# Gated cross-attention and ternary FFN: tokens of six batches read channel first and normalised in place, output weight issued by ScalarE, products and bank reads listed separately

## The chip, the cores and the metric

The program runs on one core of one Trainium2 chip. The metric is device microseconds (us) of one execution: the median of 3 runs, 726.65 us before the change (724.81 to 727.16). The profile is one further execution of the same kernel, which took 723.52 us, 721.7 us of them inside the recorded span.

Engines: PE (TensorE, matmuls; PEld is its weight load), DVE (VectorE), ACT (ScalarE), POOL (GpSimd) and SP (SyncE, which here only issues transfers). Each engine takes its instructions in order. [...]

## What is computed

Eight batches of 512 tokens with 512 channels go through two residual steps.

```python
x = x + tanh(g_xattn) * xattn(layernorm(x), ctx, mask, Wq, Wk, Wv, Wo, ...)
x = x + tanh(g_ffn) * ffn(layernorm(x), gate_w, val_w, out_w, ...)

# xattn: 16 heads of 32 channels, 64 context tokens per batch
q, k, v = proj(hs, Wq, bq), proj(at, Wk, bk), proj(at, Wv, bv)
probs = softmax(clip(mask(q @ k.T / sqrt(32))))
delta = layernorm(clip(rs, 0, 0.3) * ((probs @ v) @ Wo.T + bo)) * ln_gamma + ln_beta

# ffn: 512 -> 2 x 2048 -> 512; activations rounded to 8 bits per token, weights to -1, 0, 1
h = silu(bit_linear(x, gate_w)) * bit_linear(x, val_w)
out = bit_linear(h, out_w)
```

## The kernel before

The 4096 tokens are 32 tiles of 128 tokens; batch b has four (ST = 4). The common path (`common_path`) is one straight program. The lists of calls in `opening`, `attend_third`, `attend` (batches 3 to 6), `attend_last` and `closing` set the order, and `in_order` (L75) fixes it: on each engine, instructions stand exactly as the calls issued them. The sequencers wait for semaphores only.

Stages of the attention of batch b (counted from 0):

- `load_x` (L136) loads a tile of x, tokens on partitions. `ln1_stats` (L200) takes mean and variance per token on DVE and 1/sqrt on POOL.
- `ln1` (L222) writes the normalised tile `hs` on DVE (L230) and adds the output shift to x on POOL (L220). `ln1_turn` (L237) turns `hs` to channels on partitions: four PE transposes through the identity into one PSUM bank (L247), and one ACT copy into `hT` (L248). `hT` has one buffer for 512 tokens.
- `queries(b, o)` (L252): four f32 products from `hT` into a bank, then ACT writes `qT` (L263).
- `scores(b, a)` (L276): eight small products into four banks (L288), then ACT takes Exp of each into `prob` (L297). Exp and Silu each have to be loaded into ACT's table when it last did the other.
- `sums` (L303) adds the probabilities on PE (L311); ACT copies them (L317), and SP sends them through DRAM to 128 rows (L319, L321). `spread` (L324) takes the reciprocal on DVE and sends it through DRAM into `R` (L331, L337).
- `values` (L342): products (L351), then DVE multiplies by `R` (L358). `project_out(b, t)` (L370): four f32 products into a bank (L375), then four DVE instructions (L382 to L386). `add_delta` (L388) scales and adds into x.

Stages of the FFN of one tile: `ffn_stats` (L546), in six steps for a batch; `ffn_in` (L603) rounds a tile and turns it by a transposing DMA (L611); `ffn_mid(b, i, jj)` (L615), half of the hidden width: 4 bias products and 16 products into four banks (L625, L630), then Silu on ACT (L636) and a product on DVE (L637) for each of two column blocks; `ffn_quant` (L650), the row maximum on DVE (L655); `ffn_quant2` (L668), which rounds on ACT and DVE (L673, L674) and turns by two transposing DMAs (L679); `ffn_out` (L682): 16 products into one bank (L690), a DVE instruction (L697) and the store (L698). `tile_in`, `tile_mid`, `tile_max`, `tile_quant` and `tile_out` do the next of these for the tiles in order, so the FFN of batch b-1 runs between the attention stages of batch b.

The eight banks are two pools of four: `four` for `ffn_mid`, and `bank` for nearly all else. A bank is given on when its reader has finished. All transfers are issued by SP, the ternary weights among them: `ternary_load` (L437) brings 1 MB quarters of the gate, value and output weight during the opening, five buffers in all; `magnitude` sums them and `ternary` (L479) makes -1, 0 and 1 of them on ACT (L489, L490) or DVE (L493, L494).

## Time and profile before

| what | us |
|---|---|
| median of 3 runs | 726.65 |
| profiled execution, whole | 723.52 |
| its span | 721.7 |
| PE busy in the span | 693.5 |
| DVE / ACT / POOL busy | 519.2 / 372.0 / 133.4 |
| first matmul starts | 4.33 |
| first `ffn_mid` of the kernel starts | 132.82 |
| `attend` for one of batches 3 to 6 | 83 |
| last matmul ends | 716.05 |

In the profile, part 1 gives the busy time of each engine. The timeline lists an engine's instructions in order of time, runs of equal ones merged, and in square brackets how long the engine was idle just before and what released it. The chain of waits is followed back from the last instruction. The granted TensorE clock was 1.00 in every stretch up to 690 us and 0.96 after it.

### The profile page before, as it was taken

To read this page: it belongs to the slowest core of one execution; us is meant where nothing else is said; L and a number is where in the kernel's file an instruction comes from. 1 tells how busy PE (TensorE), PEld (TensorE's weight loads), DVE (VectorE), ACT (ScalarE), POOL (GpSimd) and SP (SyncE) were. 2 spreads that over 40 slices of the span, in tenths; PEclk is the share of its full clock that TensorE was granted. 3 is DMA by queue.
4 is the path that set the end of the run, shared out by engine and by line. 5 is a ranking of instruction groups with operands and counts; after the bars stand their busy time and mean duration, and the time that the engine had idled before them with its cause. 6 is when DMAs were issued, how large, how long until landed. Compare 5 with 4: busy or idle time off the path is not lost.

```text
span 721.7 us, 9373 instructions
## 1 busy us (share of the span) xinstructions
PE 693.5 (96%) x3292; PEld 288.6 (40%) x3292; DVE 519.2 (72%) x973; ACT 372.0 (52%) x477; POOL 133.4 (18%) x195
## 2 busy tenths in 40 slices
PE   7999899989999999999999999999999899999996
PEld 3544344334443434443443434443443334433343
DVE  3578879877687757685767957686676659888773
ACT  0569855567137663268326583077524652355551
POOL 1072303114011510043001321024000021003000
PEclk9999999999999999999999999999999999999999
DMA  8975612123322433124530525113320332233543
GB/s 275 407 245 198 208 33 88 25 67 98 88 44 56 108 76 96 36 40 96 106 84 12 106 61 132 37 38 76 86 63 15 70 97 44 53 86 75 88 80 93
DMA packets 114249, 68.36 MB, mean 95 GB/s; under 512 B 97489, under 2 KB 97489, under 8 KB 113169
## 3 DMA queue, kind: packets, MB, share of 16 engines
q1 hardware_dynamic: 114192, 67.67, 36.4%
q8 instruction: 28, 0.46, 0.3%
q14 instruction: 29, 0.23, 0.1%
HBM read 36.71 MB, written 8.91 MB: 63 GB/s over the span
## 4 chain that ended last, share of the span: by engine, by line
PE 55%; DVE 15%; issue 3%; DMA 2%; ACT 1%; POOL 1%; SPq 0%; DVEq 0%; ACTq 0%
PE four L630 19%; PE bank L690 12%; PE bank L375 10%; PE bank L258 6%; DVE h_g L655 3%; DVE h L637 2%; PE bank L630 2%; PE bank L311 2%; PE four L625 2%; DVE ln_st L558 1%; DVE x L399 1%; DVE hs L230 1%; PE bank L288 1%; PE bank L351 1%; DVE ln_st L211 1%
## 5 line engine op out<-in xcount | busy, mean ns | idle before, releaser
L636 ACT ACTIVATE gate<-four,sgv 128x512 f32<-128x512 f32 x112 | 74.9, 683 | 138.1 <-PE four L630 137.8
L630 PEld LDWEIGHTS <-xqT 128*128 128x128 bf16 x1024 | 94.9, 98 | 124.2 <-issue 15.8
L673 ACT ACTIVATE h<-h,magic,h_s 128x1024 f32<-128x1024 f32 x64 | 75.9, 1234 | 92.8 <-DVE h_s L662 92.8
L690 PE MATMUL bank<-out_tern,hqT 128*128 128x512 fp8e4 x512 | 115.4, 379 | 6.6 <-DMA hqT<-hq 3.3
L375 PE MATMUL bank<-wo_sb,cT 128*128 128x512 f32 x256 | 113.9, 596 | 3.9 <-DVE cT L358 3.2
L630 PE MATMUL four<-gate_tern,xqT 128*128 128x512 fp8e4 x448 | 115.6, 381 | 1.4 <-DMA xqT<-xq 1.4
L258 PE MATMUL bank<-hT,wq_sb 128*128 128x512 f32 x256 | 115.9, 600 | 0.4 <-ACT hT L248 0.4
L630 PE MATMUL four<-val_tern,xqT 128*128 128x512 fp8e4 x448 | 115.0, 379 | 0.0
L637 DVE SCALAR_TENSOR_TENSOR h<-four,sgv,gate 128x512 f32<-128x512 f32 x112 | 81.0, 746 | 28.1 <-PE four L630 21.4
L690 PEld LDWEIGHTS <-hqT 128*128 128x128 bf16 x512 | 49.9, 98 | 70.7 <-issue 9.8
L375 PEld LDWEIGHTS bank<-wo_sb,cT 128*128 128x128 f32 x256 | 48.1, 190 | 63.5 <-issue 51.5
L258 PEld LDWEIGHTS bank<-hT,wq_sb 128*128 128x128 f32 x256 | 47.2, 190 | 64.0 <-issue 55.6
L655 DVE TENSOR_REDUCE h_g<-h 128x1 f32<-128x2048 f32 (+1 forms) x32 | 71.6, 2238 | 0.3
L664 POOL TENSOR_TENSOR so<-h_g,unit 128x1 f32<-128x1 f32 x32 | 6.6, 205 | 297.9 <-DVE h_g L660 288.0
L220 POOL TENSOR_TENSOR x<-x,bet_bc 128x512 f32<-128x512 f32 x32 | 46.2, 1464 | 69.3 <-DVE hs L230 44.5
L674 DVE TENSOR_SCALAR hq<-h 128x1024 bf16<-128x1024 f32 x64 | 43.3, 693 | 21.4 <-ACT h L673 20.1
L569 POOL TENSOR_TENSOR x<-x,ob_bc 128x512 f32<-128x512 f32 x32 | 40.0, 1282 | 44.2 <-ACT h L568 44.2
L382 DVE TENSOR_TENSOR d<-bank,bo_bc 128x512 f32<-128x512 f32 x32 | 22.0, 687 | 26.8 <-PE bank L375 26.8
L263 ACT ACTIVATE qT<-bank,bq_sb 128x512 f32<-128x512 f32 x32 | 22.0, 688 | 36.0 <-PE bank L258 36.0
L697 DVE SCALAR_TENSOR_TENSOR o<-bank,so,x 128x512 f32<-128x512 f32 x32 | 24.0, 749 | 20.9 <-PE bank L690 18.3
L609 DVE TENSOR_SCALAR xq<-h 128x512 bf16<-128x512 f32 x32 | 13.5, 423 | 33.7 <-ACT h L606 33.7
L606 ACT ACTIVATE h<-h,magic,ln_r 128x512 f32<-128x512 f32 x32 | 25.7, 807 | 13.8 <-DVE ln_r L583 13.8
(137 smaller groups left out, 740.2 us busy)
## 6 DMA issues: line engine op xcount, KB each, us to landing
x<-in_x SPq DMA_DIRECT2D x32, 256.0 KB
R<-over SPq DMA_DIRECT2D x64, 128.0 KB
out_x<-o SPq DMA_DIRECT2D x32, 256.0 KB
wraw<-in_gate_w SPq DMA_DIRECT2D x4, 1024.0 KB
wraw<-in_val_w SPq DMA_DIRECT2D x4, 1024.0 KB
wraw<-in_out_w SPq DMA_DIRECT2D x4, 1024.0 KB
cT_in<-in_cxT SPq DMA_DIRECT2D x4, 256.0 KB
wk_sb<-in_wk SPq DMA_DIRECT2D x4, 256.0 KB
```

Of the source, the lines that this page charges most:

```text
L220: nc.gpsimd.tensor_tensor(src, src, bet_bc, ALU.add)
L258: nc.tensor.matmul(ps, wq_sb[:, c, o * P : (o + 1) * P], hT[:, c, :], start=(c == 0), stop=(c == DC - 1),)
L375: nc.tensor.matmul(ps, st_[b, "cT", c][:, t * P : (t + 1) * P], wo_sb[:, c, :], start=(c == 0), stop=(c == DC - 1),)
L569: nc.gpsimd.tensor_tensor(xs, xs, ob_bc, ALU.add)
L606: nc.scalar.activation(h2, h2, AF.Identity, scale=s[:, i : i + 1], bias=magic)
L630: nc.tensor.matmul(ps, xqT[:, c, :], w[:, c, cols], start=False, stop=(c == DC - 1))
L636: nc.scalar.activation(gate, four[2 * k], AF.Silu, scale=sgv[:, 0, i : i + 1])
L637: nc.vector.scalar_tensor_tensor(h[:, cols], four[2 * k + 1], sgv[:, 1, i : i + 1], gate, ALU.mult, ALU.mult)
L655: nc.vector.tensor_reduce(gx, h if part is None else h[:, F // 2 :], AX.X, ALU.max, apply_absolute_value=True)
L673: nc.scalar.activation(h[:, cols], h[:, cols], AF.Identity, scale=s, bias=magic)
L674: nc.vector.tensor_scalar(hq, h[:, cols], MAGIC, None, ALU.subtract)
L690: nc.tensor.matmul(ps, hqT[:, c % (FC // 2), :], weights["out"][:, c, :], start=(c == 0), stop=(c == FC - 1),)
```

## The change

- **Tokens channel first.** The kernel has a further input, `xT`, x with channels ahead of tokens. For batches 2 to 7 (the third to the eighth) `ln1` and `ln1_turn` are gone. `load_turned(b)` loads `hT` straight from `xT` by four transfers of 256 KB. `ln1_stats` keeps mean and 1/sqrt side by side (one small DVE copy more). `ln1_rows(b)` writes them to DRAM as two rows of 512, and reads each back into all 128 partitions. `ln1_turned` subtracts the mean row from `hT` on DVE in one instruction of 128x2048, `ln1_turned_end` multiplies by the other row on POOL in two of 128x1024. x itself is still loaded, for statistics and residual. Batches 0 and 1 are transposed as before.
- **Second queue.** The four 1 MB quarters of `out_w` are issued by ACT; everything else stays on SP.
- **Reads apart from products.** Nearly every helper that issued products and read their banks is split in two (`queries` and `queries_end`, `scores` and `scores_end`, `ffn_mid` and `ffn_gate`, `ffn_out` and `ffn_end`, and so on; `ffn_quant2` takes one half at a time), and all lists of calls are written anew, the start of the kernel and `closing` too.

```diff
+    def ln1_rows(b):
+        rows = dram.tile([2, S], F32, tag="lnrows", name="lnrows")
+        nc.sync.dma_start(
+            out=rows.rearrange("r (t p) -> p r t", p=P), in_=st_[b, "ln1"][1]
+        )
+        for i in range(2):
+            row = work.tile([P, S], F32, tag="hs", name="row", bufs=2)
+            nc.sync.dma_start(out=row, in_=rows[i].partition_broadcast(P))
+            st_[b, "row", i] = row
+
+    def load_turned(b, queue=nc.sync):
+        hT = st_[b, "hT"] = work.tile([P, DC, S], F32, tag="hT", name="hT")
+        for c in range(DC):
+            queue.dma_start(
+                out=hT[:, c, :], in_=xT[c * P : (c + 1) * P, b * S : (b + 1) * S]
+            )
+
+    def ln1_turned(b):
+        hT, m = st_[b, "hT"], st_[b, "row", 0].unsqueeze(1)
+        nc.vector.tensor_tensor(hT, hT, m.to_broadcast([P, DC, S]), ALU.subtract)
+
+    def ln1_turned_end(b):
+        hT, r = st_[b, "hT"], st_[b, "row", 1].unsqueeze(1)
+        for h in range(2):
+            half = hT[:, h * DC // 2 : (h + 1) * DC // 2, :]
+            nc.gpsimd.tensor_tensor(half, half, r.to_broadcast([P, DC // 2, S]), ALU.mult)
...
-            nc.sync.dma_start(
+            (nc.scalar if name == "out" else nc.sync).dma_start(
                 out=raw.rearrange("p (c n) -> p c n", c=per),
```

The list of `attend(b)` afterwards, one line for each stretch:

```python
add_scaled(b-1, 0, 1); tile_mid; sums(b, 0); queries(b, 2); sums_end(b, 0); tile_gate
queries_end(b, 2); tile_in; spread(b, 0); add_scaled(b-1, 2, 3); spread_end(b, 0)
load_turned(b+1); queries(b, 3); tile_mid; ln1_rows(b+1); tile_gate; tile_max
queries_end(b, 3); values(b, 0); values_end(b, 0); tile_mid; tile_gate; scores(b, 1)
ffn_stats(b-1, 0); ffn_stats(b-1, 1); scores_end(b, 1); tile_quant; tile_quant; tile_out
load_x; tile_in; tile_mid; tile_end; tile_gate; ln1_turned(b+1); ln1_turned_end(b+1)
tile_max; sums(b, 1); tile_out; sums_end(b, 1); ffn_stats(b-1, 2); tile_mid; tile_end
tile_gate; spread(b, 1); tile_quant; load_x; ffn_stats(b-1, 3); tile_quant
queries(b+1, 0); queries(b+1, 1); queries_end(b+1, 1); queries_end(b+1, 0)
ffn_stats(b-1, 4); ffn_stats(b-1, 5); tile_in; tile_mid; spread_end(b, 1); tile_gate
tile_max; tile_out; tile_end; values(b, 1); load_x; values_end(b, 1); tile_quant; tile_mid
tile_quant; scores(b+1, 0); ln1_stats(b+2, 0); add_beta(b+1, 0..3); project_out(b, 0)
scores_end(b+1, 0); tile_gate; load_x; project_out(b, 1); project_end(b, 0); tile_in
ln1_stats(b+2, 1); tile_out; pair_up(b+1); tile_end; ln1_stats(b+2, 2); project_end(b, 1)
tile_mid; tile_gate; project_out(b, 2); tile_max; project_end(b, 2); project_out(b, 3)
tile_quant; tile_quant; project_end(b, 3); check_sums(b); delta_scale(b); ln1_stats(b+2, 3)
```

`add_scaled` and `delta_scale` are `add_delta` in two parts. `scores(b+1, 0)`, which opened the next `attend` before, now stands ahead of `project_out(b, 0)`.

## The prediction, as it was recorded

> **What bounds the kernel now.** First the busy times in part 1 of the page, which tell which engine can set the end:

> ```profile
> PE 693.5 (96%) x3292; PEld 288.6 (40%) x3292; DVE 519.2 (72%) x973; ACT 372.0 (52%) x477; POOL 133.4 (18%) x195
> ```

> PE is idle for 28.2 of 721.7 us, 4.3 of them ahead of its first matmul and 5.7 behind its last. So the kernel gets shorter by what leaves PE's list and by stalls between matmuls, and by little else. I therefore read PE's waits next (total us, times, longest):

> ```profile
> PE bank L690 <- DMA hqT<-hq: 3.3, 2, 2.5
> PE bank L375 <- DVE cT L358: 3.2, 2, 2.0
> PE bank L690 <- ACT x L297: 2.2, 1, 2.2
> PE bank L247 <- DVE o L697: 1.9, 4, 0.5
> PE bank L247 <- DVE hs L230: 1.6, 3, 1.0
> ```

> The two L247 lines are the transposes' own waits. Then the groups by shape (busy, mean ns | idle before):

> ```profile
> L311 PE MATMUL bank<-prob,ones 64*32 64x512 f32 x208 | 20.7, 600 | 0.0
> L247 PE MATMUL bank<-ident,hs 128*128 128x128 f32 x128 | 18.3, 279 | 4.1 <-DVE o L697 1.9 <-DVE hs L230 1.6 <-ACT qT L263 0.3
> ```

> A transpose takes 18.3 / 128 = 0.143 us of PE. The line of the sums hides something: the list of waits has none for it, yet the timeline of PE over one attend (start, us) shows two lengths for the same 16 products:

> ```profile
> 308.54 1.09 PE L311 MATMUL bank<-prob,ones 64*32 64x512 f32 x16
> ...
> 326.99 0.66 PE L247 MATMUL bank<-ident,hs 128*128 128x128 f32 x4 [0.48 <-DVE o L697]
> ...
> 336.39 2.73 PE L311 MATMUL bank<-prob,ones 64*32 64x512 f32 x16
> ```

> The second, 2.73 against 1.09, is a stall of 1.64 that counts as busy. ACT's timeline says why: the scores end at 332.5, but ACT comes to their Exps late, and these last until 338.0:

> ```profile
> 333.92 1.28 ACT L297 ACT_TABLE_LOAD   x1
> 335.22 2.78 ACT L297 ACTIVATE prob<-bank,esh,esc 128x512 f32<-128x512 f32 x4
> ```

> Last, one stretch of one period of the attention (start:end, length, then busy time of PE, PEld, DVE, ACT, POOL):

> ```profile
> 303.79:386.96 83.17, 82.69 (x408) 34.26 (x408) 58.77 (x114) 42.46 (x57) 15.90 (x23) 1.00 0.35 73
> ```

> The other engines have 24 us or more to spare in each period. There are four such, so a us in each is worth four.

> **Transposes.** Six batches lose 16 each: 96 x 0.143 = 13.7 of busy time. In a period the records overlap their neighbours (three spans of 1.04, 0.66 and 0.66 take 2.12 between starts), so 6 x 2.12 = 12.7; I take **-13**. Their waits leave with them: 1.9 (o), 1.3 of 1.6 (hs; the rest is in batches 0 and 1) and 0.3 (qT): **-3.5**. After them the same out follows a mid, whose 3.9 us let DVE finish o, so nothing takes their place.

> **The norm that replaces them.** Off PE: it loses on ACT four copies (L248) of 0.59, and on DVE four L230 of 0.54. It gains:
> - Four loads of 256 KB per batch, in place of none. They stand on SP's queue and wait for the last queries of batch b, which read the one hT. Behind them on SP stand the two rows' transfers and the next transposes of hq, which are due some 11 us later. An issue takes SP 0.43, 1.7 for four; DMA is busy 0.35 of the period. Cost: nothing; if the cover were gone, 1.7 per batch.
> - The rows: a write of 1,024 pieces of 4 bytes, which the trace does not show, then reads. Nearest are SP's waits for the rows of sums and of reciprocals, 30.7 / 16 = 1.9 in the mean and 6.3 at most. The subtract comes about 17 us after; I take 1.9 and nothing at either end.
> - One subtract of 128x2048 on DVE. Below: four L230, 2.1; above: four L386 (two tensors read, 0.752), 3.0. I take 2.25, nearer to L230; DVE's sum is then as before.
> - Two POOL products of 128x1024. L220 has two inputs from SBUF and ranges 1.26 to 3.32 for 512: 4 x 1.27 = 5.1 at the least, 4 x 3.32 = 13.3 at the most. I take 5.1, as L220's median is 1.36.

> When is hT needed? On PE, the sums (1.0), an out (3.5) and a mid (3.9) stand between the mid ahead of the subtract and the queries of b+1: 8.4. The chain is the gate's last DVE product (0.86), subtract (2.25) and products (5.1): 8.2. The second half is needed only 1.7 later. So **0**, with little slack for the first half and 2 for the second.

> [...]

> **Sums apart from scores.** In the new list an out and a mid (7.4 us) stand between scores(b, 1) and sums(b, 1), so Exp has ended: 4 x 1.64 = **-6.6**. But an out then directly follows the scores, and scores(b+1, 0) are directly followed by project_out(b, 0). Scores fill all four banks of their pool, so the next product waits until the first Exp has read its bank. The row that shows such a case is in the last attention:

> ```profile
> 574.14 3.61 PE L690 MATMUL bank<-out_tern,hqT 128*128 128x512 fp8e4 x16 [2.19 <-ACT x L297]
> ```

> Below, the wait is 0.9: Exp starts 0.2 after the scores' end (304.66 to 304.86) with the table loaded ahead, and one takes 0.70. Above, the table load (1.28) and a tile's rounding (2.37) stand before it: 4.6. In the list both ACT entries ahead are a gate's Silu, as at 304.86, so I take 1.0 for each: two in each of four attends, one in the third, 9 x 1.0 = **+9**. In the last attention the 2.19, and 0.9 by which the scores ahead are slow (1.95 in place of 1.11), become 2.0: **-1.1**.

> **Single waits.** The first out waits 2.54 for hqT at 156.84; it moves behind a mid (3.9): **-2.5**. The cT wait of 1.20 at 595.1 goes, as another product is put between: **-1.2**.

> **The opening and the second queue.** The other cT wait, 2.0 at 86, follows a transfer of R that landed 6.3 late behind 2 MB of output weight issued just ahead of it. With the weight on ACT it is issued at other times: **-1** (between 0, when it lands among the same transfers, and -2). ACT pays 0.4 to 0.5 for each issue, and may wait at its head for the ternary value weight; Exps stand behind. In the opening ACT is the less loaded, so 0.

> [...]

> **Sum:** -13 - 3.5 - 6.6 + 9 - 1.1 - 2.5 - 1.2 - 1 = -19.9. From the profiled 723.5 that gives 703.6; the median shown lies 3.1 above that execution, so 706.8. I say **706**. By stage: each attend 83.2 to 81 (-2.1 of transposes, -0.5 of waits, -1.64, +2), the third 6 less, the opening 1 to 3 less.

> **Rivals.**
> - *A, the Exp is late.* At one scores of each attend ACT still has the table load and a rounding ahead, as at 333.92: 3.65 more each, 4 x 3.65 = +14.6: 720. For it: the old list shows just that at the second half, and DVE makes the gates late. Against: in the new list the roundings stand behind scores_end. 0.18; spans 712 to 724.
> - *B, slower: the norm is late.* If the POOL pair is near its 13.3, the chain is 0.86 + 2.25 + 13.3 = 16.4 against 8.4 + 1.7 of cover: 6.3 per batch, x 6 = 38: 744. With the chain 3.4 beyond the cover, a pair of 10.4, it costs 20 and decides; above that the kernel is slower. For it: the 3.32 of L220, and DVE 70% busy. Against: the median of 1.36. 0.12.
> - *C, nothing.* B at that point, a pair of 10.4: the norm gives back just what the transposes and stalls gave, 726. 0.04.
> - *D, more.* The waits for banks are hidden, +9 gone: 697. PE's other idle between matmuls is 28.2 - 4.3 - 5.7 = 18.2, of which the steps above take 9.3; were the rest gone too, 688. 0.06.

> **Chances.** Forecast 0.60 (699 to 712), A 0.18, B 0.12, C 0.04, D 0.06. A difference below 0.3% (2.2 us) is about what a measurement of this kernel cannot tell from none. Faster: 0.60 + 0.18 + 0.06 = 0.84; within 0.3%: 0.04; slower: 0.12. The range takes the forecast, most of A and half of D: 694 to 722.

> **What would show it.** Right: L247 falls to 32 instructions; the period is about 81; the sums take 1.09 throughout; PE's list has an L690 and an L375 line released by Exp (L297 before), about 1.0 each; queries wait for POOL under 0.3. Wrong: queries wait for POOL's products by several us (B), the bank waits are 3 or more (A), or PE waits in the opening for weights that ACT issued late, which I put at nothing.

## The result and the profile after

The changed kernel takes 751.88 us in the median (751.42 to 759.47, 4 runs) against 725.73 us: 1.0383 of the time, 95% interval 1.0314 to 1.0452. I had forecast 706, range 694 to 722. The profiled execution took 751.72 us, with a span of 749.9 us against 721.7.

Part 1 of its page, and the lines of PE's waits that matter (total us, times, longest):

```profile
PE 690.7 (92%) x3196; PEld 280.4 (37%) x3196; DVE 537.2 (72%) x961; ACT 361.1 (48%) x453; POOL 168.0 (22%) x207
```

```profile
PE bank L757 <- DMA hqT<-hq: 14.7, 5, 4.1
PE bank L331 <- DVE cT L417: 10.5, 1, 10.5
PE bank L433 <- DVE cT L417: 4.9, 2, 4.2
...
PE bank L757 <- ACT prob L344: 4.3, 5, 0.9
PE bank L433 <- ACT prob L344: 3.6, 4, 0.9
```

PE lost 96 transposes, yet it is busy for only 2.8 us less, and idle for 59.2 us in place of 28.2. The two lines released by `prob` are the nine bank waits that the prediction counted, 7.9 in place of 9. The first two lines, 25.2 us, are what it did not have. L757 is an out (the products of `ffn_out`), L331 a scores, and `hqT` and `R` (for `cT`) are brought by transfers.

So the next view is the list of what SP's queue waited for:

```profile
SPq L749 <- DVE hq L744: 72.7, 27, 9.1
SPq L229 <- DMA lnrows<-ln_r: 57.0, 6, 11.8
```

L229 reads the rows back. It waits six times, 9.5 us in the mean, for the write of the 1,024 numbers that stands just ahead (L224). SP's queue in one attention (start, us) shows who stands behind it:

```profile
339.41 0.38 SPq L224 DMA_DIRECT2D lnrows<-ln_r  x1
348.57 0.80 SPq L229 DMA_DIRECT2D row<-lnrows  x2
349.48 4.93 SPq L749 DMA_TRANSPOSE hqT<-hq  x2
```

The write is issued at 339.4, the reads can go at 348.6, and only then come the two turns of hq (transposing transfers into hqT), which take 4.9 to issue beside half a MB of rows. DVE writes the two halves of hq at:

```profile
347.74 0.69 DVE L744 TENSOR_SCALAR hq<-h 128x1024 bf16<-128x1024 f32 x1 [0.34 <-ACT h L743]
348.87 0.69 DVE L744 TENSOR_SCALAR hq<-h 128x1024 bf16<-128x1024 f32 x1 [0.43 <-ACT h L743]
```

So here the first half had been ready for 1.1 us when its turn was issued; in the other three attentions it was 2.1, 4.5 and 3.5. In the two attentions where hq had waited least, the pair of turns took 4.9 and 4.6 to issue, against 2.6 or 2.7 for most pairs of the kernel before. hqT is late by both: the wait, and the half MB that it puts right ahead of the turns. On PE, from one scores of the period to the next, with the sums and the out that needs hqT:

```profile
298.50 1.11 PE L331 MATMUL bank<-qT,kT 32*64 32x512 f32 x16
...
342.54 1.22 PE L331 MATMUL bank<-qT,kT 32*64 32x512 f32 x16
...
352.05 1.09 PE L358 MATMUL bank<-prob,ones 64*32 64x512 f32 x16
355.65 5.31 PE L757 MATMUL bank<-out_tern,hqT 128*128 128x512 fp8e4 x16 [2.51 <-DMA hqT<-hq]
...
383.89 1.11 PE L331 MATMUL bank<-qT,kT 32*64 32x512 f32 x16
```

The sums now take 1.09, as forecast. The out waits 2.51, and then takes 5.31 in place of 3.6: from 356 to 358 us the granted clock is 0.50, from 358 to 360 it is 0.69. Without these 4.2 us the period, 85.4 between the scores at 298.50 and at 383.89, would be 81.2.

In the third attention the same wait holds up the second transfer of batch 2, R:

```profile
151.42 0.39 SPq L224 DMA_DIRECT2D lnrows<-ln_r  x1
160.26 0.80 SPq L229 DMA_DIRECT2D row<-lnrows  x2
161.15 2.43 SPq L392 DMA_DIRECT2D R<-over  x4
```

```profile
159.53 1.07 PE L331 MATMUL bank<-qT,kT 32*64 32x512 f32 x4
171.08 2.59 PE L331 MATMUL bank<-qT,kT 32*64 32x512 f32 x12 [10.48 <-DVE cT L417]
```

The values of batch 2 hold two banks until R is there, so the scores stand still for 10.5 us.

By stage, in us, as differences from the kernel before (first column), with the kernel of the experiments that turns the statistics on PE (called "turned rows" below) in the last column. The forecast's terms are put to the stages here; for the third attention the prediction itself had said "6 less".

| stage | before | forecast | after | turned rows |
|---|---|---|---|---|
| start to the first `ffn_mid` | 132.8 | -3.1 | +5.7 | +5.3 |
| to the scores of batch 3 | 87.7 | -5.5 | +10.2 | -1.6 |
| to the last scores | 349.5 | -9.0 | +11.2 | -7.4 |
| to the end of the span | 151.7 | -2.3 | +1.1 | -0.5 |
| sum | 721.7 | -19.9 | +28.2 | -4.2 |

### The profile page after: what moved, and what is told of

Read it like the earlier page. It is cut to its first block, busy times and chain, and to the rows that moved or that the text cites. A ratio compares the mean times of both kernels' runs of the same rounds, so it can differ in the third digit from the quotient of the medians.

```text
span 749.9 us, 9162 instructions
## 1 busy us (share of the span) xinstructions
PE 690.7 (92%) x3196; PEld 280.4 (37%) x3196; DVE 537.2 (72%) x961; ACT 361.1 (48%) x453; POOL 168.0 (22%) x207
## 4 chain that ended last, share of the span: by engine, by line
PE 72%; DMA 12%; DVE 9%; ACT 3%; issue 2%; SPq 1%; POOL 1%; DVEq 0%; ACTq 0%
PE four L696 24%; PE bank L757 14%; PE bank L433 12%; PE bank L295 9%; DMA hqT<-hq 4%; PE bank L696 3%; PE four L691 2%; PE bank L780 2%; PE bank L331 2%; DMA R<-over 2%; DMA rows<-den 1%; PE bank L794 1%; PE bank L406 1%; DMA lnrows<-ln_r 1%; DMA wo_sb<-in_wo 1%
## 5 line engine op out<-in xcount | busy, mean ns | idle before, releaser
L757 PE MATMUL bank<-out_tern,hqT 128*128 128x512 fp8e4 x512 | 125.2, 401 | 21.9 <-DMA hqT<-hq 14.7
L707 DVE SCALAR_TENSOR_TENSOR h<-four,sgv,gate 128x512 f32<-128x512 f32 x112 | 81.2, 747 | 68.6 <-PE four L696 38.7
L757 PEld LDWEIGHTS <-hqT 128*128 128x128 bf16 x512 | 51.8, 102 | 99.4 <-issue 30.2
L744 DVE TENSOR_SCALAR hq<-h 128x1024 bf16<-128x1024 f32 x64 | 50.7, 806 | 15.2 <-ACT h L743 12.4
L261 POOL TENSOR_TENSOR x<-x,bet_bc 128x512 f32<-128x512 f32 x32 | 50.2, 1597 | 18.2 <-DVE bet_bc L177 17.5
L255 POOL TENSOR_TENSOR hT<-hT,row 128x1024 f32<-128x1024 f32 x12 | 28.4, 2388 | 79.4 <-DVE hT L247 69.7
L344 ACT ACTIVATE prob<-bank,esh,esc 128x512 f32<-128x512 f32 x40 | 27.9, 778 | 21.0 <-PE bank L331 21.0
L196 POOL TENSOR_TENSOR ln_r<-ln_r,mhalf 128x4 f32<-128x4 f32 x16 | 16.5, 1032 | 80.8 <-DVE ln_r L195 46.5
## 6 DMA issues: line engine op xcount, KB each, us to landing
wraw<-in_gate_w SPq DMA_DIRECT2D x4, 1024.0 KB, 12.2
```

The costliest lines, as they stand in the source:

```text
L255: nc.gpsimd.tensor_tensor(half, half, r.to_broadcast([P, DC // 2, S]), ALU.mult)
L261: nc.gpsimd.tensor_tensor(src, src, bet_bc, ALU.add)
L707: nc.vector.scalar_tensor_tensor(h[:, cols], four[2 * k + 1], sgv[:, 1, i : i + 1], gate, ALU.mult, ALU.mult)
L744: nc.vector.tensor_scalar(hq, h[:, cols], MAGIC, None, ALU.subtract)
L757: nc.tensor.matmul(ps, hqT[:, c % (FC // 2), :], weights["out"][:, c, :], start=(c == 0), stop=(c == FC - 1),)
```

## The experiments

**Theory W:** the write of 1,024 pieces holds SP at the reads' wait, and what is queued behind is late. Rivals: T, traffic of rows and xT; L, the new lists; A, the output weight on ACT. (These letters, and Q, E and R below, are not the prediction's rivals A to D.)

### Rows read later

```diff
+        ln1_rows_end(b + 1)      # the two reads, now behind the turns of hq
         tile_out()
```

> The changed kernel with one move: the reads of the two rows are issued by SP later, behind the turns of hq (in the opening behind the sums of batch 1), the write stays where it is. Theory W (SP stands 8.3 to 11.8 us at the reads' wait for the write of 1,024 pieces, and all that is queued behind it is late): the stall of 10.5 at 160 goes, the four waits for hqT (13.3 in all) fall under 1 each, the half clock after them goes; 700 to 712 us. Rival T (not the wait, but the rows' and xT's traffic keeps hqT and R late): the reads still run beside the turns; over 735. Rival L (the new lists themselves put outs ahead of their hqT): over 730, the stall at 160 stays.

Measured: 733.09 us, 1.0102 of before (1.0061 to 1.0143). The waits for hqT in the attentions are gone and the period is 81.7, but the stall in the third attention is still 6.7, and the one ahead of the first projection is 5.6, and the time is over the 700 to 712 expected. W is half right. The trace tells what it lacked:

```profile
152.04 0.39 SPq L224 DMA_DIRECT2D lnrows<-ln_r  x1
153.04 1.71 SPq L398 DMA_DIRECT2D R<-over  x4
```

R was issued 1 us behind the write and ahead of the reads, so SP did not stand at the write first. Its last part still landed 12.7 us after its issue (2.9 in the median of those that the trace shows), while the view of the transfers shows 0 to 55 GB/s until 163.6 us. So in this run the write delayed transfers, not only the queue.

### The write in 128 pieces

```diff
-            out=rows.rearrange("r (t p) -> p r t", p=P), in_=st_[b, "ln1"][1]
+            out=rows.rearrange("r (p k) -> (r p) k", k=2 * ST),
+            in_=st_[b, "ln1"][1].rearrange("p r t -> p (r t)"),
```

> The changed kernel with the write of mean and 1/sqrt in 128 pieces of 32 bytes in place of 1,024 of 4, so the rows hold the numbers at wrong places; all else, the order of issue too, stays. Theory W: SP's wait for the write falls from 9.5 in the mean to about 2, as the 128-row write of the reciprocals has it; the stall at 160 falls to 2 to 4, the waits for hqT below 2 each; 708 to 722 us. Rival T (traffic of the rows' reads): bytes are the same, over 740. If the write's length has to do with something else than the pieces, SP's wait stays over 6.

Measured: 715.99 us, 0.9831 (0.9796 to 0.9866). SP's line answers to the one above:

```profile
SPq L230 <- DMA lnrows<-ln_r: 18.7, 6, 4.7
```

3.1 each in place of 9.5, with the same 4 KB, issued in the same place: 36 us of the kernel hang on how they are cut into pieces. (Number and size of the pieces change together here, so the runs do not tell which of the two counts.) T falls as the main cause, and the period is 81.1, which was the forecast's.

### Output weight on SP again

```diff
-            (nc.scalar if name == "out" else nc.sync).dma_start(
+            nc.sync.dma_start(
```

> The changed kernel with the four quarters of the output weight issued by SP again. Theory W: the opening is late through the rows, so this gives 750 to 755 us, first half of the FFN within 2 us of 138.6. Rival A (the opening lost its 5.7 us to transfers that ACT issues at bad times): 744 to 748, the first half of the FFN near 133.

Measured: 757.8 us, 1.0414 (1.0362 to 1.0466), the FFN beginning at 143.2, 4.6 later. Rival A falls. In the profiles the weight on ACT is 6.1 us better in these lists; the two intervals overlap, so the gain may be less. What is lost moves: with the weight on SP, R of batch 0 lands 2.6 us after its issue in place of 5.5, and PE waits 0.5 in place of 4.2 ahead of the first projection, but 5.3 for ACT's copies of sums behind it.

### The norm left out

```diff
     def ln1_rows(b):
-        if b >= B:
+        if b >= 0:
             return
```

and the same in `ln1_turned` and `ln1_turned_end`: no write, reads, subtract or products in the six batches.

> The changed kernel without write and reads of the rows, subtract and products in the six batches: tokens enter the queries there unnormalised. Theory W: what is left is the gain alone, 698 to 708 us, no stall at 160, no hqT wait over 1. Rival L (lists): over 725. Against e1 it gives the price of the norm when it is late for nobody: under 4 us by W.

Measured: 718.48 us, 0.9888 (0.9847 to 0.993). That is no faster than the norm with a short write: beside that, subtract and POOL's products cost nothing that can be measured. But it is 12 us above my forecast, and the FFN begins at 137.5. So part of the miss is neither write nor norm: in the attention, with a period of 81.1, rival L falls, but the opening's loss belongs to the new lists or to the loads that they place.

### Statistics turned on PE, written in 8 pieces

```diff
+        ps = bank()
+        nc.tensor.transpose(ps[: 2 * ST, :P], st_[b, "ln1"][1].rearrange("p r t -> p (r t)"), ident)
+        flat = work.tile([P, S], F32, tag="hs", name="flat", bufs=2)[: 2 * ST, :P]
+        nc.scalar.copy(flat, ps[: 2 * ST, :P])
-        nc.sync.dma_start(out=rows.rearrange("r (t p) -> p r t", p=P), in_=st_[b, "ln1"][1])
+        nc.sync.dma_start(out=rows.rearrange("r (t p) -> (r t) p", p=P), in_=flat)
```

In the third and the common attention `ln1_rows` also moves ahead of the mid that stood before it. The runs built on this kernel have this move too.

> The changed kernel with the eight statistics of a token turned by one PE transpose of 128x8, copied by ACT, and written as 8 pieces of 512 bytes; rows hold the right numbers. One PE instruction and one ACT copy more per batch. Theory W (SP's wait for the write of 1,024 pieces was the loss): as the 32 byte write, 714 to 719 us, SP's wait for the write 2 to 3 each, period of the attention 81.1 to 81.4. If the extra bank or copy stalls PE or ACT: over 722.

Measured: 720.04 us, 0.9894 (0.9877 to 0.9910): the fastest version with the right numbers in the rows, and faster than both kernels. SP waits 18.1 / 6 = 3.0 for the write, the period is 81.5. It is 4 us above the write in 128 pieces, 1 beyond what I expected; in the profiles the two are 1.6 apart, 1.3 of it in the opening.

### The second queue alone, in the kernel before

```diff
-            nc.sync.dma_start(
+            (nc.scalar if name == "out" else nc.sync).dma_start(
```

> The kernel before with one change, the four quarters of the output weight issued by ACT. My prediction's step: 1 us less (0 to 2). Rival A, ACT's waits for weight buffers hold back its Exps in the opening: 2 to 6 us more. 724 to 727 by mine, 729 to 733 by A.

Measured: 745.86 us, 1.0249 (1.0227 to 1.0270). Its rival A was right in kind, and the loss is three times its upper end. PE and ACT:

```profile
PE four L288 <- ACT qT L263: 16.7, 1, 16.7
```

```profile
ACT wraw L489 <- DVE val_tern L494: 20.1, 1, 20.1
```

The issues need buffers that DVE frees, ACT's own work stands still for 20 us behind two of them, and behind them on ACT stand qT and the Exps. In the changed lists ACT has no such wait: its four issues go out between 63.3 and 74.9 us, beside its other work. So the second queue's price lies in its place in the list.

### Transposes back in the common attention

Batches 4 to 7 with `ln1` and `ln1_turn` again, and without the loads of hT, the rows, the subtract and the products:

```diff
-        ln1_turned(b + 1)
-        ln1_turned_end(b + 1)
+        ln1(b + 1, 0, 1)
         tile_max()
         sums(b, 1)
         tile_out()
         sums_end(b, 1)
+        ln1_turn(b + 1, 0, 1)
+        ln1(b + 1, 2, 3)
```

> The kernel with turned rows, but batches 4 to 7 are normalised token first and transposed on PE as before, in the new lists (no loads of hT, rows, subtract or products for them). It prices transposes in the new order: by my prediction 2.1 per batch plus waits of 0 to 0.6, so 8.5 to 11 us over the kernel with turned rows, a period of 83.2 to 83.8. If what was gained in the period came from the new order alone, the two are within 3 us. If the chain of turns is late for the queries, the difference is over 14.

Measured: 729.43 us, 1.0032 (1.0015 to 1.0049), 9.4 over turned rows; the period is 83.9 in place of 81.5. The price of the transposes, 2.1 and their waits per batch, was right.

### Where the opening lost

Three kernels move the output weight towards or behind R of batch 0; of each the lines shown are the main ones. First, in turned rows, three quarters late, and the first sum of magnitudes behind a projection:

```diff
-        ternary_load("out", 0)
         ternary("val", 1, True)
-        ternary_load("out", 1)
...
-        ternary_load("out", 2)
+        ternary_load("out", 0, 1, 2)    # behind spread_end(0, 1)
```

> The kernel with turned rows, the first three quarters of the output weight issued only after the second R of batch 0 (5 to 14 us later). Theory R: in the opening PE waits for R, whose two landings are late behind these 3 MB; then the stall of 4 to 5 ahead of the first output projection falls under 1, the FFN begins near 133 in place of 137, 711 to 714 us. Rival: the weight's sums on DVE come late in its place and the FFN begins no earlier, 715 to 722.

Measured: 722.3 us, 0.9939 (0.9917 to 0.9962). ACT does not wait for SP: it issued at 72.9, SP issued R at 74.4, and cT could start at 86.5, as in turned rows (86.7). Then the whole weight behind ACT's copies of the sums of batch 1, and the first two sums of magnitudes behind projections:

```diff
         sums_end(1, 0)
+        ternary_load("out", 0, 1, 2, 3)
```

> The kernel with turned rows, all four quarters of the output weight issued by ACT only behind its copies of the sums of batch 1, when R of batch 0 has been issued, and their sums of magnitudes moved behind the projections. In the run with three quarters late ACT still came 1.4 us ahead of SP and R landed 12.2 us after its issue behind 4 MB. Theory R (PE waits ahead of the first projection for R, which stands behind the output weight): R lands within 4 us, the stall of 4.5 at 83 falls under 1.5, the FFN begins at 132 to 135 in place of 138, 713 to 717 us. If DVE's work on the weight, now 8 us later, holds back the scales of the FFN instead: FFN at 138 or later, 719 to 726 us.

Measured: 728.95 us, 1.0043 (1.0028 to 1.0059). The stall ahead of the first projection is gone:

```profile
83.37 14.00 PE L437 MATMUL bank<-wo_sb,cT 128*128 128x512 f32 x32 [0.48 <-ACT den L372]
```

It was 4.46, and 16.34 for the same 32 products, in turned rows. So R was late behind the weight. But the FFN begins at 147.7: the sums of the weight's magnitudes then come late (PE waits 5.8 for them, L543 released by `acc`). Last, the place between, about 1 us behind R, with the rows read late in the attentions (the next kernel but for the opening):

```diff
         ln1_rows_end(2)
+        ternary_load("out", 0, 1, 2, 3)
```

> The kernel before this one, with the four quarters of the output weight issued by ACT some 1 us behind R of batch 0, 10 to 11 us later than the first was, and their sums a little later. Earlier runs showed R late behind the weight (stall of 4.5), and DVE late when the weight came another 6 to 15 us later. If there is a place between: stall at 83 under 1.5 and the FFN begins at 133 to 136, 711 to 715 us. If the opening is bound by the weight's own way (load, magnitudes, mean), the FFN begins at 138 to 142 whatever R does, 718 to 724 us.

Measured: 733.28 us, 1.0107 (1.0073 to 1.0142), 7.3 over the next kernel, which it is to be compared with; a stall of 6.0 and the FFN at 140.7. R's four issues, from 74.3, took 7.5 us in place of 1.7, so by my reading the weight still got between them. No place that I tried wins.

### Turned rows, read late

```diff
         tile_quant()
+        ln1_rows_end(b + 1)
         tile_out()
```

in turned rows, in the third and the common attention.

> The kernel with turned rows and 8 pieces, and in the third and the common attention the rows read behind the turns of hq. If the reads' half MB still keeps hqT late (three waits, 2.7 us, in the kernel with turned rows), these go under 1: 715 to 718.5 us against 720. If the rows then come late for the subtract, queries wait for POOL: 720 or more. If neither: 719 to 721.

Measured: 725.99 us, 0.9989 (0.9973 to 1.0005). A miss: the waits for hqT only fall from 2.7 to 2.2, and those for xqT rise from 1.5 to 6.6, since the turn of the next xq now stands behind the reads. I had also misread the 2.7: only one of the three waits, 0.77, is in an attention (it stays, at 0.78); the two others are in the closing, which this edit does not touch. So rival T has this share: in this run the half MB delayed what stood next (xqT, 5.1 us more).

### The write issued by ACT

```diff
-        nc.sync.dma_start(
+        nc.scalar.dma_start(
             out=rows.rearrange("r (t p) -> p r t", p=P), in_=st_[b, "ln1"][1]
```

> The kernel with the rows read later, and in it the write of 1,024 pieces issued by ACT in place of SP; nothing else. In the kernel with late reads a transfer of R that SP issued 1 us behind that write landed 12.7 us later, against 2.9 in the median, while next to no bytes moved. Theory Q (transfers of one issuing engine stand in line behind the write): R of batch 2 lands in 3 to 5 us, the stall of 6.7 at 161 falls under 1.5; 714 to 722 us. Theory E (the write of small pieces holds the 16 DMA engines, whoever issues): R lands 9 or more us late as before, the stall stays over 5, 728 to 734 us.

Measured: 751.8 us, 1.0347 (1.0315 to 1.0378). Theory Q falls. ACT's issue of the write, SP's own write of the reciprocals and the reads of R behind it:

```profile
153.80 0.37 ACTq L224 DMA_DIRECT2D lnrows<-ln_r  x1
155.69 0.33 SPq L388 DMA_DIRECT2D over<-rden  x1
163.19 3.30 SPq L398 DMA_DIRECT2D R<-over  x4
```

R's issue waits 7.5 us for a write of 16 KB. Over the kernel SP's ten waits for such writes grew to 41.0 us, from 13.9 with the rows read late and the long write on SP:

```profile
SPq L398 <- DMA over<-rden: 41.0, 10, 7.9
```

E's own signs did not come either: R landed 2.8 us after its late issue, and the stall was 4.4. What was held is the write ahead of R, and it costs more than E expected: the period is 85.6 to 86.7 in place of 81.7, and the first projection waits 11.1. From 150 to 180 us the packets that ACT issued stand on a queue of their own (1,040 on q10), and yet SP's waits are 41.0 in place of 13.9: in this run another issuing engine was no other path. Whether the 16 engines or the memory behind them are held, these runs do not tell.

## Why the prediction was wrong

- **The rows, where it failed.** "I take 1.9 and nothing at either end", with 6.3 as upper end. The write of 1,024 pieces took 8.7 to 12.2 us. My nearest rows were waits for writes of at most 128 pieces, and I took their mean as if pieces did not count. (I also mixed two rows: 30.7 / 16 is the sums' alone, whose longest is 4.8; the reciprocals' are 25.8 / 16 = 1.6, and 6.3 is theirs.) The trace shows the pieces: from 151 to 163 us, with this write and one of 128 pieces, it has 1,184 packets under 512 bytes.
- **"Behind them on SP stand ... due some 11 us later".** True, and so nothing was left: in the attention shown 9.2 of 11 went to the wait, and the reads' half MB took the rest. I named the queue behind the loads, but asked only of the loads how long they hold it. In the third attention R stood there, which I did not name. These two points are most of the 48 us between forecast and result (19.9 + 28.2, by the profiles): with a short write the kernel is 36 faster.
- **The half clock, not counted at all.** After three of the four waits for hqT in the attentions (13.3 us) the granted clock was 0.53, 0.50 and 0.50 for the next 3 us, and the out took 5.31, 6.24 and 5.28 in place of 3.62, 6.0 us more. (Behind the fourth, 3.17, the clock stayed at 1.00, see the last section.)
- **Transposes.** Right: 2.4 per batch in the attention with their waits, for 2.6.
- **Sums, bank waits.** Right: 1.09 in all sums but one of the opening; nine waits of 0.86 to 0.89. (Ahead of the late Exps at 333.92 stood four instructions of the FFN's statistics, L568, 2.55, and not a rounding, as rival A has it.)
- **The norm's chain on DVE and POOL.** Right that it costs nothing when the rows come in time. The subtract took 2.29 (2.25 taken), a POOL product 2.35 in the median and 2.81 at most (5.1 for the pair). Rival B had the right sign for the wrong reason.
- **The opening.** Wrong by 7 to 9 us, write or not. The first projection starts when R of batch 0 has landed and DVE has made cT of it: cT could start at 85.3 to 87.0 in six of the seven kernels of these lists with the weight early on ACT and the long write not there too (85.4 before). So the transposes taken out ahead of it gave nothing. The wait that the -1 was to take away grew from 2.0 to 4.2. The 6.3 that it was read from was SP's wait for the write of the reciprocals, at 74.7 to 81.1; R itself was issued only then. Behind the scores of batch 1 the sums now come at once, a bank wait (0.89, then 2.0 hidden in the sums) that I did not count. The stall (4.5 in turned rows) is followed by a granted clock of 0.50 for 3 us, 2.3 on the projections. What else keeps the first `ffn_mid` late is open.
- **The third attention.** 4 of the 5.5 forecast are missing even with turned rows: scores wait for banks that the values hold until R (scores 2.1 longer), and an out waits 0.8 for hqT's second half; the last 1.0 is not traced.
- **Second queue, 0 for ACT.** Right in the new lists, for no good reason: I had named the wait for the ternary value weight and put nothing on it, and in the old lists just that wait, 20 us of ACT, costs 18. No row of the kernel before gave its size: SP's waits for `gate_tern` (12.8 us) are at issues of the value weight, which stayed on SP.
- **The last attention's -1.1.** Did not come: 2.19 again, and in the changed kernel the out behind it took 5.30.

## What to carry to other kernels

Look at the pieces of a transfer, not only at its bytes: a write of 1,024 single numbers took longer (8.7 to 12.2 us) than the half MB read back behind it (3.8 to the one landing that the trace shows), and held back others (R landed 12.7 us after its issue behind it, against 2.9 in the median). When a step puts a wait into an in-order queue, list what stands behind that wait, with due times, also for the transfers that the step itself adds. Work taken off an engine is worth nothing where a transfer ends last, as in this opening.

## What the runs showed of the hardware

- 1,024 pieces of 4 bytes took 8.7 to 12.2 us from their issue to the issue that waits for them; 128 pieces of 32 bytes 3.1 in the mean, 8 of 512 bytes 3.0. While the long write runs and the loads issued ahead of it are done, the transfer view of the changed kernel shows next to nothing moved (339 to 349 us, 40 slices, tenths of busy and GB/s):

```profile
DMA  8989989989999942000000000000000000000000
GB/s 229 303 270 262 295 287 295 311 320 361 418 321 186 79 19 2 0 0 0 0 0 0 0 0 0 0 0 0 0 0 0 0 0 0 0 0 0 0 0 0
```
